# A graph network on one core: the features of layer 0's first convolution turned through HBM, and the plan ordered anew

## The chip, the cores and the metric

The kernel runs on one core of a Trainium2 chip. The metric is device time in microseconds (us), the median of several runs; lower is better. The core has a matrix engine (TensorE, "PE" in the profile; "PEld" is its loading of weights), a vector engine (VectorE, "DVE"), a scalar engine (ScalarE, "ACT"), GpSimd ("POOL"), and a queue engine (SyncE, "SP") that issues most transfers. Each engine works through its own instructions in order, and waits at semaphores for the others.

## The reference

Sixteen graphs of 1024 nodes with 128 features each pass through four layers. Each layer normalises its input, takes `relu` of it, computes a graph operation with the dense 1024 x 1024 adjacency, and adds the result to its input. All is float32.

```python
def _adapt_conv(h, edge_weight, W, b, is_last):      # layer 0: three of these in a row
    h = h @ W + b
    norm = jnp.linalg.norm(h, axis=-1, keepdims=True)
    nh = h / jnp.maximum(norm, EPS)
    cos = jnp.einsum('bij,bkj->bik', nh, nh)
    ew = edge_weight * cos
    h = jnp.einsum('bpq,bqc->bpc', ew, h)
    if not is_last:
        h = jax.nn.relu(h)
    return h
```

Layer 1 multiplies the features by the adjacency and applies two dense matrices. Layer 2 is an attention whose scores are the `tanh` of a sum of two numbers, one of each node. Layer 3 is an attention whose scores come from a product of features with features, symmetrised, masked by the adjacency, with a softmax, and three gates after it.

## The kernel before

**Tiles.** A graph's 1024 nodes are 8 blocks of 128. The features lie with nodes on the partitions (`h`, 128 x 1024: 8 blocks side by side), and, where TensorE has to contract over features, turned, with features on the partitions (`hT`, `hTn`, `hnT`). `hT` is what a convolution's projection `h @ W` reads (`project`, groups `psP`); `hTn` is the turned `h`, both sides of the product `cos` (groups `sq`).

**Turning features** is done in two ways. `flipped` (line 1221 on) transposes 4 blocks at a time on TensorE into a bank of PSUM (`flip`, line 1164), and ScalarE copies the bank to SBUF (`evict`, line 1217): 8 transposes and 2 copies for a graph's features. `squares` (line 1168 on) does it without TensorE: one DMA stores the features in HBM (512 KB), four DMAs (one for each group of 32 partitions) fetch them so that every 32 x 32 square lies where its transpose belongs, and one VectorE instruction transposes the squares in place:

```python
        op("DMA", 3.6, [d], [dst], fetch, lat=2.4)
        dve(V(N), [dst], [dst], lambda: nc.vector.transpose(dst.t[:, 0:N], dst.t[:, 0:N]), True)
```

Before the change, layer 0's normalised input is turned by `squares` in graphs 2 to 15, layer 3's in graphs 1 to 13; all of layer 0's `hTn` are turned by `flipped`, three in a graph.

**The square product.** `Square` computes only the upper triangle of `cos`, row by row (8 rows, 2 halves each: `sq`). ScalarE keeps blocks of it (`above`, line 1387), and TensorE transposes them into the rows below (line 1365). In the middle graphs the quarter that lies furthest below the diagonal comes through HBM instead (`send`): VectorE transposes 32 x 32 squares (line 1377), a DMA stores two rows of blocks (`by_hbm`), four fetch them at their places (`got`). VectorE then multiplies each row by the norm and the adjacency (`ew`, line 1584), and TensorE accumulates (`acc`, lines 1417 and 1428).

**The adjacency** is loaded twice for each graph: as it stands (`adjL`) for layer 1, and turned, through the same 32 x 32 squares (`adjT`, line 1504), for the others.

**The order of the work.** Nothing is issued as the Python code runs. Every step is an `Op` with an engine, a cost, the buffers that it reads and writes, and a rank; the class `Plan` puts all steps of all sixteen graphs into one order, which is then emitted engine by engine. The rank is `batch * PERIOD + due`, with `due` from the table `TIMES`; the table names a step by layer, engine and tile ("00 PE ps": the first convolution's transposes on TensorE), with entries of their own for the first two graphs (`<0`, `<1`) and the last two (`>1`, `>0`), and one set for all others. `order` walks through time: it finds the step that can start first, and of the steps of that engine that can start within `WINDOW` of it takes the one with the lowest rank. Steps of up to `AHEAD` = 2 graphs after the oldest unfinished one may be started, so three graphs are in the works at once. `POOLS` says how many buffers there are of each sort, `KINDS` how many of them a kind of tile may hold, in all and for graphs after the oldest. The order of every engine's instructions, SP's transfers too, is therefore fixed when the program is built, and is the same from one middle graph to the next.

Of the kernel before, what the change touches and what calls it, by code (L numbers as in the profile page):

```python
# [18 lines left out]
D = 128  # L19
# [36 lines left out]
class Plan:  # L56
# [78 lines left out]
    def order(self):  # L135
# [11 lines left out]
        done, oldest = [], 0  # L147
        while ready:
# [4 lines left out]
            found = []  # L153
# [25 lines left out]
            if not found:  # L179
                stuck = [b.name for o in ready if o.batch == oldest for b in o.new]  # L180
                raise RuntimeError(f"no slot for any of {stuck}")
            first = min(found, key=lambda f: f[0])
            at, o = min(
                (f for f in found if f[1].engine == first[1].engine and f[0] <= first[0] + self.window),
                key=lambda f: f[1].rank,
# [35 lines left out]
def tile_adj_preln(  # L221
# [30 lines left out]
    B = x.shape[0]  # L252
# [9 lines left out]
    FLAGS = set("CabcdkxhyzTGmrHWMD3")  # L262
# [61 lines left out]
    for load_it in first:  # L324
# [13 lines left out]
        "adjT": ("adjT", 16, 16), "adjL": ("adjL", 5, 5), "x": ("x", 3, 3), "w4": ("big", 9, 6),  # L338
        "chunk": ("big", 9, 8), "above": ("above", 2, 2), "got": ("got", 1, 1), "ps": ("bank", 6, 7),
        "acc": ("bank", 6, 8), "small": ("small", 9, 12), "row": ("row", 2, 4), "hbm": ("hbm", 3, 2),  # L340
        "hrow": ("hrow", 2, 1), "mask": ("mask", 5, 5), "dot": ("dot", 10, 8),
    }
    PERIOD, AHEAD, WINDOW = 144.89, 2, 0.05

    TIMES = {
        "T DMA raw <0": [45.7, -38, -16.15, 49.25, 9.05, 10.9, 32.75, 4.4],
        "T PE raw <0": [6.9, 8.55, 10, 14.35, 31.1, 9.5, 16.55, 15.55, 20.15, 29.15, 25.45, 37.8, 42.75,
            38.2, 41.55, 44.35],
        "T ACT adjT <0": [8.65, 14, 10.4, 13.35, 16.4, 15.35, 19.25, 20.5, 24.5, 31.15, 33.75, 39, 40.6,
            41.5, 42.7, 45],  # L350
        "T DVE su <0": [52.25],
        "x DMA x <0": [45.65, -6.9],
        "0 DVE st <0": [5.1, 5.15],
        "0 DVE mv <0": [7.1],
        "0 POOL rstd <0": [8.05],
        "0 DVE nb <0": [9.85],
        "0 DVE hn <0": [9.9],
        "0 ACT hn <0": [14],
        "0 PE ps <0": [11.15, 11.3],
        "0 ACT hT <0": [9.25, 12.15],  # L360
        "00 PE psP <0": [33.35, 27.4],
        "00 DVE h <0": [14.25, 12.85],
        "00 PE ps <0": [15.25, 16.1],
        "00 ACT hTn <0": [16.35, 17.25],
        "00 ACT sq <0": [15.5, 19.1],
        "00 DVE ss <0": [15.65, 13.1, 14],
        "00 POOL rn <0": [19.5],
        "00 PE sq <0": [-5, 18.3, 16.7, 19.75, 11.5, 20.4, 14.65, 23.15, 33.4, 31.25, 7.35, 35.7, 33.35,
            37.35, 43.9, 44.5, 41.1, 42.65, 44.4, 43.4, 46.85, 50.85],
        "00 ACT above <0": [19.15, 22.8, 21.35, 22.05, 26.55, 25.8, 31.25, 34.7, 39.05, 45],  # L370
        "00 DVE ew <0": [21.45, 23.5, 21.35, 27.95, 26.1, 24.4, 27.8, 32.75, 38.1, 37.65, 36.45, 43.6, 45.35,
            49.5, 51.65, 54.95],
        "00 PE acc0 <0": [22.5, 43.85, 23.7, 25.85, 30.2, 29.2, 31.65, 31.95, 37.65, 39.45, 47.5, 52.7, 56.2,
            52, 66, 57.2],
        "00 POOL params <0": [24.3, 29.3, 33.35, 36.35, 43.25, 47.85, 33.2],
        "00 DMA params <0": [61.4],
        "00 DVE params <0": [64.75, 67.4, 70.15, 85.4, 74.55],
        "00 PE params <0": [66.15, 67.95, 73.25],
        "00 ACT hT <0": [58.75, 57.25],
        "01 PE psP <0": [54.9, 58.45],  # L380
        "01 DVE h <0": [75.3, 78.3],
        "01 PE ps <0": [81.6, 78.7],
        "01 ACT hTn <0": [77.4, 78.4],
        "01 ACT sq <0": [77.25, 77.9],
        "01 DVE ss <0": [79, 80.5, 81.8],
        "01 POOL rn <0": [81.95],
        "01 PE sq <0": [79.6, 81.15, 81.35, 82.85, 82, 80.95, 84.25, 83.4, 91.3, 87.25, 87.6, 90.65, 91.05,
            95.35, 96.35, 96.45, 95.45, 100.65, 101.75, 96.05, 102.9, 103.05],
        "01 ACT above <0": [81.4, 81.55, 86.1, 87.45, 85, 83.2, 87.3, 92.15, 98.35, 101.95],
        "01 DVE ew <0": [85.3, 83.45, 84.6, 85.3, 86.25, 88.95, 88.25, 89.9, 92.55, 92.5, 96, 96.25, 92.05,  # L390
            102.9, 97.2, 103.55],
        "01 PE acc0 <0": [80.2, 85.15, 89.3, 85.15, 91.9, 92.8, 93.45, 93.7, 94.5, 99.15, 97, 102.1, 101.35,
            103.8, 102.25, 104.9],
        "01 ACT hT <0": [101.95, 110.3],
        "02 PE psP <0": [105.75, 103.9],
        "02 DVE h <0": [107.35, 108.3],
        "02 PE ps <0": [108.45, 108.35],
        "02 ACT hTn <0": [109, 111.65],
        "02 ACT sq <0": [107.85, 109.6],
        "02 DVE ss <0": [110.25, 110.9, 110.4],  # L400
        "02 POOL rn <0": [113.3],
        "02 PE sq <0": [112.75, 113.5, 114.4, 119.4, 115.05, 119.85, 119.1, 119.35, 123.15, 122.15, 121.3,
            129.65, 125.8, 128.95, 127.85, 133.25, 126.35, 130.55, 133.1, 121.6, 133.1, 132.85],
        "02 ACT above <0": [114.15, 115.55, 116.15, 115.7, 117.85, 121.6, 120.6, 122.3, 130.4, 132.1],
        "02 DVE ew <0": [114.9, 115.55, 117.6, 118.45, 119.95, 119.55, 122.7, 122.8, 125.7, 129.1, 129.8,
            131.05, 110.6, 135.15, 124.75, 128.75],
        "02 PE acc0 <0": [114.95, 117.95, 120.2, 117.3, 125.7, 127.15, 125.35, 133.65, 126.15, 130.35, 136,
            133.45, 139.25, 135.55, 138.7, 136.1],
        "02 DVE x <0": [134, 137.25],
        "T DMA adjT <1": [-121.95, -133.95, -119.1, -112.25, -140.55, -203.7, -102.2, -133.55],  # L410
        "T DVE adjT <1": [-117.5, -112.15, -108.9, -105.1, -100.5, -89.9, -92.65, -88.65],
        "T ACT adjT <1": [-114.75, -105.3, -107.95, -101.4, -98, -62.65, -86.35, -86.05],
        "1 DVE st <0": [140.75, 141.25],
        "1 DVE mv <0": [143.55],
        "1 POOL rstd <0": [143.15],
        "1 DVE nb <0": [145.8],
        "1 DVE hn <0": [141.7],
        "1 ACT hn <0": [147.25, 147.4],
        "1 DVE x <0": [160.65, 167.6, 169.75],
        "1 DMA adjL <0": [58.65, 63.6, 66, 162.05, 89.6, 149.8, 153.1, 154.2],  # L420
        "1 DVE adjL <0": [87, 75.3, 80.25, 90.3, 81.9, 154.55, 159.15, 169.4],
        "1 PE acc1 <0": [147.9, 148.75, 149.6, 150.6, 151.35, 152.45, 155, 153.5, 156.1, 144.25, 158.5,
            157.4, 159.55, 156.6, 160.1, 163.85],
        "1 ACT g <0": [161.65, 162.5],
        "1 PE py <0": [163.05, 164.6, 165, 164.15],
        "1 ACT y1 <0": [163.5, 163.25, 168.05, 164.1],
        "1 PE py2 <0": [157.3, 166.9],
        "2 DVE st <0": [169, 170.15],
        "2 DVE mv <0": [172.3],
        "2 POOL rstd <0": [173.3],  # L430
        "2 DVE nb <0": [174.9],
        "2 DVE hn <0": [172.65],
        "2 ACT hn <0": [176.55, 179.7],
        "2 PE ps <0": [205.85, 174.4],
        "2 ACT hnT <0": [180.85, 180.1],
        "2 DVE alone <0": [57.7],
        "2 DVE x <0": [179.05, 214.1, 221.35],
        "2 PE psP <0": [180.65, 182.15, 187.2],
        "2 ACT h <0": [206.2, 185.8, 182.6],
        "2 DVE hrow <0": [183.15],  # L440
        "2 PE pf <0": [185.5],
        "2 ACT hfl <0": [185.45],
        "2 PE pt <0": [199.4],
        "2 ACT sr <0": [182.75],
        "2 DMA sd <0": [186.45],
        "2 DMA s1 <0": [187.05],
        "2 DVE h <0": [184.3],
        "2 ACT e2 <0": [192.75, 195.95, 191.7, 194.45, 196.3, 200.05, 196, 198.85, 200.4, 201.9, 201.95,
            200.1, 203.75, 206.4, 209.5, 205.15],
        "2 DVE e2 <0": [196.9, 196.3, 195.65, 195.05, 199.65, 194.1, 200.3, 199.6, 201.55, 203.65, 201.25,  # L450
            202.3, 207.55, 209.4, 208.6, 208.15],
        "2 PE acc2 <0": [198.15, 201.7, 197.55, 200, 200.45, 199.35, 203, 201.85, 200.95, 203.85, 202.7,
            201.6, 201.1, 203.55, 206.3, 212.65, 207.85, 206.55, 207.15, 208.8, 211.5, 209.85, 210.05, 212.15],
        "2 DVE rden <0": [209.55, 213.7, 212.8, 214.4],
        "3 DVE st <0": [215.4, 207.25],
        "3 DVE mv <0": [210],
        "3 POOL rstd <0": [221.85],
        "3 DVE nb <0": [203.4],
        "3 DVE hn <0": [208.15],
        "3 ACT hn <0": [221.15, 224.35],  # L460
        "3 PE ps <0": [236.25, 224.2, 241.4, 227.7],
        "3 ACT hnT <0": [221.55, 224.2],
        "3 PE pg <0": [242.5, 229.05],
        "3 ACT gT <0": [225.95, 242.2],
# [1055 lines left out]
    def layer0(b, xt, aT, prepared):  # L1520
# [7 lines left out]
        rn = None  # L1528
# [594 lines left out]
```

## Time and profile before

| | |
|---|---|
| median of 3 runs | 2393.26 us (2389.92 to 2393.75) |
| the profiled execution | 2391.87 us |
| its span, first to last instruction | 2390.1 us |
| TensorE clock granted | 0.997 |
| busy: TensorE, VectorE, ScalarE, GpSimd | 2355.8, 2023.5, 1454.3, 247.2 us |
| TensorE instructions | 11689 |
| transposes of `h` into `ps_hTn` | 384, mean 276 ns each |
| HBM read, written | 220.16 MB, 77.13 MB |

Durations overlap on TensorE: a matrix product's row in the profile lasts from its start until its last result is out, while the next one has started already. A float32 product appears as two passes, a transpose as one. What a TensorE instruction takes from the engine is the distance from its start to the next one's, called pitch below.

### The profile page before, as it was taken

The numbers are of one execution on the slowest core, as the hardware profiler recorded it, in microseconds if no ns is written. First come the engines' busy times: TensorE is split into PE (matmuls) and PEld (weight loads), VectorE is DVE, ScalarE is ACT, GpSimd is POOL, SyncE is SP. The second block draws the span as 40 slices with busy tenths as digits, with TensorE's granted clock in tenths as the row PEclk, the third lists the DMA queues.
The fourth block names the chain that finished last, engine by engine and source line by source line (L and its number), as shares of the span: only waits on it lengthen the run. The fifth ranks groups of instructions, "written<-read, shape, count | busy, mean of one in ns | idle before, by whom it ended". The sixth has DMA issues, their size and how long they took to land.

```text
span 2390.1 us, 35188 instructions
## 1 busy us (share of the span) xinstructions
PE 2355.8 (99%) x11689; PEld 1565.0 (65%) x11689; DVE 2023.5 (85%) x5556; ACT 1454.3 (61%) x2589; POOL 247.2 (10%) x168
## 2 busy tenths in 40 slices
PE   8999999999999999999999999999999999999997
PEld 5568566675767657566575766757666575765764
DVE  6668798888989989898888989989899888887676
ACT  6325765756566565755756667565765756655375
POOL 3001010100101101010100101001011100100012
PEclk9999999999999999999999999999999999999999
DMA  9331938758595775948769486785957758155000
GB/s 195 86 106 45 176 89 166 152 110 173 111 170 135 132 167 117 169 114 160 158 110 182 99 170 138 128 173 108 167 131 141 161 113 159 45 89 124 11 17 18
DMA packets 1243941, 299.61 MB, mean 125 GB/s; under 512 B 1049976, under 2 KB 1225216, under 8 KB 1243760
## 3 DMA queue, kind: packets, MB, share of 16 engines
q1 hardware_dynamic: 1223600, 286.67, 60.3%
q10 hardware_dynamic: 19264, 9.70, 1.4%
q8 instruction: 92, 1.51, 0.3%
q0 software_dynamic: 896, 1.01, 0.2%
q14 instruction: 89, 0.73, 0.1%
HBM read 220.16 MB, written 77.13 MB: 124 GB/s over the span
## 4 chain that ended last, share of the span: by engine, by line
PE 93%; DVE 3%; ACT 2%; DMA 1%; SPq 1%; issue 0%; DVEq 0%; ACTq 0%
PE acc L1417 36%; PE sq L1355 20%; PE acc L1428 18%; PE psP L1195 5%; PE sq L1365 4%; PE py L1646 2%; PE py L1205 2%; PE ps_hTn L1164 1%; PE pg L1205 1%; PE psN L1195 1%; SPq L1504 1%; PE ps_h3T L1164 1%; DVE h L1239 1%; PE ps_hnT L1164 1%; DVE ew L1584 0%; DVE x L1239 0%
## 5 line engine op out<-in xcount | busy, mean ns | idle before, releaser
L1417 PE MATMUL acc<-ew,h 128*128 128x512 f32 x1024 | 481.0, 595 | 2.6 <-DVE ew L1584 2.5
L1584 DVE SCALAR_TENSOR_TENSOR ew<-sq,rn,adjT 128x512 f32<-128x512 f32 x612 | 435.5, 738 | 56.0 <-PE sq L1365 27.9
L1355 PE MATMUL sq<-hTn 128*128 128x512 f32 (+3 forms) x1152 | 435.2, 487 | 0.2 <-ACT hTn L1217 0.2
L1387 ACT COPY above<-sq 128x384 f32<-128x384 f32 (+3 forms) x432 | 166.3, 393 | 364.1 <-PE sq L1365 231.7
L1417 PEld LDWEIGHTS acc<-ew,h 128*128 128x128 f32 x1024 | 183.5, 191 | 180.2 <-issue 135.7
L1355 PEld LDWEIGHTS sq<-hTn 128*128 128x128 f32 x1152 | 197.8, 191 | 150.8 <-issue 103.0
L1428 PEld LDWEIGHTS acc<-h,ew 128*128 128x128 f32 x2048 | 245.5, 192 | 29.2 <-issue 26.0
L1428 PE MATMUL acc<-h,ew 128*128 128x128 f32 x2048 | 253.2, 275 | 0.2 <-DVE ew L1584 0.2
L1417 PE MATMUL acc<-e,hs 128*128 128x512 f32 x512 | 246.1, 597 | 2.9 <-DVE e L1890 2.9
L1428 PEld LDWEIGHTS acc<-h,e 128*128 128x128 f32 x2048 | 233.0, 192 | 15.1 <-DVE e L1758 8.7
L1428 PE MATMUL acc<-h,e 128*128 128x129 f32 x2048 | 234.3, 275 | 3.5 <-DVE e L1758 3.4
L1417 PE MATMUL acc<-adjL,hn 128*128 128x512 f32 x512 | 231.1, 593 | 0.1
L1157 POOL TENSOR_TENSOR rstd<-ve,mhalf 128x8 f32<-128x8 f32 x64 | 104.8, 1637 | 1096.2 <-DVE ve L1276 1040.6
L1849 DVE CUSTOM_DVE_ANT_0 e<-mask,sq 128x512 f32<-128x512 int8 x204 | 136.0, 680 | 91.1 <-ACT above L1387 74.7
L1515 ACT ACTIVATE adjT<-adjT 128x1024 f32<-128x1024 f32 x120 | 126.5, 1054 | 100.9 <-DVE adjT L1512 75.9
L1365 PEld LDWEIGHTS sq<-ident,above 128*128 128x128 f32 x960 | 124.0, 141 | 77.2 <-issue 54.2
L1890 DVE TENSOR_TENSOR e<-e,adjT 128x512 f32<-128x512 f32 x248 | 163.9, 682 | 11.3 <-ACT e L1881 11.1
L1365 PE MATMUL sq<-ident,above 128*128 128x128 f32 x960 | 173.3, 273 | 0.0
L1758 DVE SCALAR_TENSOR_TENSOR e<-adjT,e 128x512 f32<-128x512 f32 x256 | 162.3, 696 | 5.8 <-ACT e L1754 5.1
L1417 PEld LDWEIGHTS acc<-adjL,hn 128*128 128x128 f32 x512 | 94.8, 190 | 107.5 <-issue 92.9
L1377 DVE STREAM_TRANSPOSE above<-sq 128x512 f32<-128x512 f32 x208 | 144.7, 705 | 20.3 <-PE sq L1355 19.2
L1838 ACT ACTIVATE mask<-adjT 128x1024 int8<-128x1024 f32 x112 | 117.9, 1054 | 59.2 <-DVE peak L1849 59.0
(163 smaller groups left out, 3645.0 us busy)
## 6 DMA issues: line engine op xcount, KB each, us to landing
adjL<-in_adj_dram SPq DMA_DIRECT2D x128, 512.0 KB, 4.8
adjT<-in_adj_dram SPq DMA_DIRECT2D x480, 128.0 KB, 3.7
by_hbm<-above SPq DMA_DIRECT2D x104, 512.0 KB, 3.7
got<-by_hbm SPq DMA_DIRECT2D x416, 128.0 KB, 2.9
s<-sd SPq DMA_DIRECT2D x15, 512.0 KB, 3.7
out_dram<-z ACTq DMA_DIRECT2D x15, 512.0 KB, 4.1
d_hT<-hn SPq DMA_DIRECT2D x14, 512.0 KB, 3.2
hT<-d_hT SPq DMA_DIRECT2D x56, 128.0 KB, 3.0
```

The lines of the kernel that those rows point to most:

```text
L1195: nc.tensor.matmul(dst.t[:, (c - lo) * n : (c - lo + 1) * n], cols(srcT.t, c), w, start=True, stop=True)
L1355: lambda: nc.tensor.matmul(dst.t[:, (first - lo) * P :], cols(leftT.t, j), span(rightT.t, first, hi), start=True, stop=True),
L1365: nc.tensor.transpose(cols(dst.t, r), cols(above.t, p), ident)
L1377: lambda: nc.vector.transpose(span(above.t, p, p + 4), read.t),
L1387: lambda: nc.scalar.copy(span(above.t, p, p + hi - first), read.t[:, (first - lo) * P :]),
L1417: lambda s=s, lo=lo, hi=hi: nc.tensor.matmul(acc[s].t, cols(h.t, at, w), span(ew.t, lo, hi), start=(j == 0), stop=(j == NB - 1)),
L1428: nc.tensor.matmul(a.t[:, (c - lo) * n : (c - lo + 1) * n], cols(ew.t, c), h.t[:, at * w : at * w + n], start=(j == 0 and c == lo), stop=( ...
L1515: lambda t=t, c=c: nc.scalar.activation(t.t, t.t, AF.Copy, accum_out=su.t[:, c : c + 1]),
L1584: lambda view=view, ew=ew, rn=rn, j=j, lo=lo, hi=hi: nc.vector.scalar_tensor_tensor(by_block(span(ew.t, lo, hi), D, 4), view(), rn.t[:, j ...
L1758: lambda e=e, j=j, lo=lo, hi=hi: nc.vector.scalar_tensor_tensor(span(e.t, lo, hi), span(aT[j].t, lo, hi), 0.0, span(e.t, lo, hi), op0=ALU. ...
L1849: lambda e=e, view=view, mask=mask, peak=peak, s=s, lo=lo, hi=hi: nc.vector.tensor_tensor_reduce(by_block(span(e.t, lo, hi), D, 4), by_blo ...
L1890: lambda e=e, j=j, lo=lo, hi=hi: nc.vector.tensor_mul(span(e.t, lo, hi), span(e.t, lo, hi), span(aT[j].t, lo, hi)),
```

## The change

The first convolution's `hTn` is made by `squares` instead of `flipped` in graphs 2 to 15 (flag `n`; the test `"nop"[i] in FLAGS and b > 1` was there before). Graphs 0 and 1, and the second and third convolution of all graphs, keep `flipped`. The plan is ordered anew: other limits in `KINDS` for the planner, another `PERIOD`, all due times in `TIMES` replaced; the number of buffers (`POOLS`) is the same. Where two engines can start at the same moment the planner now takes the one that comes first in `LATENCY`. Two further flags (`w`, `K`) are named in the code and not set.

```diff
+        rows = {e: i for i, e in enumerate(self.LATENCY)}
...
-            first = min(found, key=lambda f: f[0])
+            first = min(found, key=lambda f: (f[0], rows[f[1].engine]))
...
-    FLAGS = set("CabcdkxhyzTGmrHWMD3")
+    FLAGS = set("CabcdkxhyzTGmrHWMD3n")
...
-        "adjT": ("adjT", 16, 16), "adjL": ("adjL", 5, 5), "x": ("x", 3, 3), "w4": ("big", 9, 6),
-        "chunk": ("big", 9, 8), "above": ("above", 2, 2), "got": ("got", 1, 1), "ps": ("bank", 6, 7),
-        "acc": ("bank", 6, 8), "small": ("small", 9, 12), "row": ("row", 2, 4), "hbm": ("hbm", 3, 2),
-        "hrow": ("hrow", 2, 1), "mask": ("mask", 5, 5), "dot": ("dot", 10, 8),
+        "adjT": ("adjT", 16, 16), "adjL": ("adjL", 5, 5), "x": ("x", 3, 3), "w4": ("big", 11, 5),
+        "chunk": ("big", 13, 11), "above": ("above", 2, 2), "got": ("got", 1, 1), "ps": ("bank", 8, 7),
+        "acc": ("bank", 8, 7), "small": ("small", 7, 18), "row": ("row", 5, 6), "hbm": ("hbm", 3, 3),
+        "hrow": ("hrow", 1, 1), "mask": ("mask", 5, 5), "dot": ("dot", 6, 11),
     }
-    PERIOD, AHEAD, WINDOW = 144.89, 2, 0.05
+    PERIOD, AHEAD, WINDOW = 145.06, 2, 0.05
...
-        "00 PE psP": [-87.3, -102.4],
-        "00 ACT hTn": [-83.9, -84.95],
+        "00 PE psP": [-95, -133.3],
+        "00 DMA d": [-82.95],
+        "00 DMA hTn": [-88.45],
+        "00 DVE hTn": [-68.05],
...
-        if "D" in FLAGS and b > 1:
+        if "D" in FLAGS and b > (0 if "w" in FLAGS else 1):
...
-                if "M" in FLAGS and b >= B - 2:
+                if "K" in FLAGS or "M" in FLAGS and b >= B - 2:
```

In the changed program, a middle graph's new store stands on SP between the store and the fetches of the layer 3 features of the graph two before it, and its four fetches behind those; the VectorE transpose stands behind layer 3's bias additions of that earlier graph.

## The prediction

> **What bounds the kernel now.** I read the page's busy table first, then the chain of work that ended last, then stretches of the span, then one graph row by row.
>
> ```profile
> PE 2355.8 (99%) x11689; PEld 1565.0 (65%) x11689; DVE 2023.5 (85%) x5556; ACT 1454.3 (61%) x2589; POOL 247.2 (10%) x168
> ...
> PE 93%; DVE 3%; ACT 2%; DMA 1%; SPq 1%; issue 0%; DVEq 0%; ACTq 0%
> ```
>
> TensorE carries 93% of the chain. The chain in order of time shows the same piece at the same place of every middle graph:
>
> ```profile
> 616.86 14.29 PE acc L1428 x128
> ...
> 761.14 14.29 PE acc L1428 x128
> ```
>
> So a middle graph takes 761.14 − 616.86 = 144.28 us. The view by stretches (us, then busy PE, PEld, DVE, ACT, POOL, clock, DMA share, GB/s) tells where TensorE is not busy:
>
> ```profile
> 0.00:40.00 40.00, 29.89 (x154) 20.72 (x154) 20.67 (x65) 30.54 (x63) 16.00 (x27) 1.00 1.04 206
> 40.00:184.30 144.30, 141.10 (x638) 88.28 (x639) 97.38 (x245) 45.99 (x100) 18.02 (x17) 0.99 0.46 104
> 184.30:328.60 144.30, 142.70 (x736) 96.35 (x735) 122.25 (x343) 104.09 (x177) 12.09 (x7) 1.00 0.53 111
> ...
> 616.86:761.14 144.28, 144.23 (x714) 95.60 (x713) 128.34 (x351) 90.70 (x160) 13.32 (x8) 1.00 0.71 142
> ...
> 2204.00:2390.10 186.10, 168.44 (x906) 116.79 (x905) 133.33 (x400) 106.50 (x189) 29.00 (x14) 0.97 0.05 17
> ```
>
> Of 34.3 us without TensorE work, 10.1 lie in the first 40 us, 4.8 in the next two stretches, 17.7 in the last 186 us; a middle graph has 0.05. Busy overlaps, so I count the middle graph by pitch (start to start) instead: its timeline has 188 passes of 512 columns at 0.4295 us (2.58 us for six), 402 of 128 to 131 at 0.1117 (14.29 for 128), 16 of 384 at 0.32, 16 of 256 at 0.215, and 89 transposes. The transposes' pitch:
>
> ```profile
> 657.91 1.04 PE L1164 MATMUL ps_h3T<-ident,h 128*128 128x128 f32 x8
> 658.78 1.02 PE L1205 MATMUL pg<-hnT,wg 128*128 128x512 f32 x2
> ```
>
> Eight take 658.78 − 657.91 = 0.87 us, 0.109 each. The sum is 80.7 + 44.9 + 5.2 + 3.4 + 9.7 = 143.9 us: of 144.28, only 0.3 to 0.4 us is waiting. In the middle, TensorE work is the time.
>
> **What the Trainium skill says.** "TensorE: Matmul & The Clock Gate", Part 4: PE-mode transpose, gives about 275 ns for a 128x128 transpose inside a kernel. The trace agrees as to duration (276 ns below), but its pitch is 109 ns, and only the pitch leaves the bound. "Perfetto Trace Analysis", Identifying the Most-Contended Engine, says the same: busy share is no good measure for TensorE. "VectorE: DVE Perf Modes", The three transpose paths: VectorE transposes within 32x32 blocks only, so the blocks must be moved by DMA; that is what the trace's `hT` does. "DMA: Bandwidth & Descriptors", Anatomy of one DMA: some 2 us fixed, mostly completion; here 2.4 to 4.0 us to landing.
>
> **The change part by part.** The group that it cuts, and the existing twin of what it adds (last line: us from issue to landing):
>
> ```profile
> L1164 PE MATMUL ps_hTn<-ident,h 128*128 128x128 f32 x384 | 55.9, 276 | 3.2 <-DVE h L1542 2.6
> ...
> L1217 ACT ACTIVATE hTn<-ps_hTn x96: 578/597/625, 16.3 to 2231.3; 128x512 f32<-128x512 f32 x96
> ...
> L1186 DVE STREAM_TRANSPOSE hT<-hT x14: 1232/1235/1237, 110.8 to 2071.6; 128x1024 f32<-128x1024 f32 x14
> ...
> DMA to landing us min/median/max: 2.4/3.0/4.0
> ```
>
> - *TensorE.* 384 transposes are 16 graphs x 3 convolutions x 8. The first convolution of 14 graphs goes: 112 transposes x 0.109 = 12.2 us less. The rest of its instructions is the same in number.
> - *ScalarE.* 28 evictions x 0.597 = 16.7 us less, on an engine busy 61%: worth nothing by itself.
> - *VectorE.* 14 x 1.235 = 17.3 us more. A middle graph goes from 128.3 to 129.6 of about 143.4 us, 90%. In the changed order it stands just before layer 3's first row of graph b−2, where VectorE now idles 2.11 us for a ScalarE copy (658.94 + 0.16 to 661.21). Worth nothing while that hole stays; if the cover goes, at most 1.24 us a graph.
> - *SP and DMA.* Per graph one store of 512 KB and four fetches of 128 KB. SP now:
>
> ```profile
> 627.28 0.38 SPq L1173 DMA_DIRECT2D d_hT<-hn  x1
> 630.50 2.45 SPq L1181 DMA_DIRECT2D hT<-d_hT  x4
> 644.88 0.38 SPq L1173 DMA_DIRECT2D d_hnT<-hn  x1
> 648.14 2.29 SPq L1181 DMA_DIRECT2D hnT<-d_hnT  x4
> 650.62 0.77 SPq L1397 DMA_DIRECT2D by_hbm<-above  x1
> ```
>
> The new store stands between `d_hnT` and the fetch of `hnT`, in the 2.9 us in which SP only waits for `d_hnT` to land: free. The new fetches stand behind `hnT`'s and hold up the send of graph b−1's third square by about 2.4 us, to some 653 us on this clock. But the new order issues both sends of that square before either fetch; now the second send (657.29) waited behind the first fetch. By these rows the second fetch then ends issuing near 662 instead of 663.3: no loss.
>
> *Is the round trip hidden?* The new chain: projection done near 644.8, `h` added on VectorE by 645.8, store, `hnT`'s fetches to 650.4, its own to 652.8, 3.0 us to land: 655.8. Two consumers. The VectorE transpose: in the changed order VectorE has between the second `h` addition and it 3 reductions x 0.68, 4 block transposes x 0.71, 8 scalings x 0.7, `hnT` 1.24, three additions of 1.5 together and a small one: about 13.5 us, so it is reached near 659.3, 3.5 us after the data. The first square on TensorE: the pitches of what stands between the projection and it add to 36.9 us in every graph from 3 to 13 (38.8 before, transposes included), far more than 12 to 15. Graph 2 has 75, graphs 14 and 15 have 38 and 44.
>
> - *The new order.* Slots are the same, the planner's limits and due times are new. Other covers, in pitch, middle graph before and after: smallest from a square's row to the accumulation that uses it 1.8 and 1.6 us (second smallest 2.2 and 1.7); from layer 2's last accumulation to layer 3's projection 23.95 and 25.68. One shrinks where there is little: the first convolution, from the last row sent through HBM to the first accumulation that needs it back, 13.1 and 12.2 us. Now:
>
> ```profile
> 731.93 1.41 DVE L1584 SCALAR_TENSOR_TENSOR ew<-got,rn,adjT 128x512 f32<-128x512 f32 x2
> ...
> 733.38 1.02 PE L1417 MATMUL acc<-ew,h 128*128 128x512 f32 x2
> ```
>
> The scaling is done at 731.93 + 0.75 = 732.7 and its product used at 733.38: some 0.5 us over, with a hand-over of 0.2 us, if the data landed only just before. With 0.9 us less cover, up to 0.4 us a graph is lost in 12 graphs: 0 to 5 us, or nothing if the data landed earlier. I take 1. At both ends the order differs in detail; the last 33 us of TensorE work (graph 14's gate projections and graph 15's layer 3) come in nearly the same order. I take zero for both ends, with 5 us either way, about a seventh of the 34.3 us there.
>
> **Sum** against the profiled execution: span 2390.1 − 12.2 + 1 = 2378.9; its own time, 1.77 longer, 2391.87 − 11.2 = 2380.7. The median of the runs is 2393.26, 1.39 above that execution, so 2382 (−0.5%). This measurement can tell about 0.2%, 4.8 us.
>
> **Rivals.**
> 1. *The gain stays, but the ends lose.* For: the start (15 us without work, waiting for loads) and the tail were planned anew, and nothing carries over from one order to another there. Against: the tail's order is nearly the old one. Loss 5 to 14 us: 2387 to 2396, about 2390.
> 2. *The new wait decides: slower.* Place: VectorE is in order, and behind the new transpose stand layer 3's first peaks and the scalings of graph b−1's fetched rows, which TensorE waits for. If `hTn` lands later than 659.3 here, VectorE stops. Each us beyond costs up to a us in each of 14 graphs; it cancels the gain at 0.87 us a graph past all cover, and shows as slower at 1.2, that is landing some 5 us later than I work out. For: DMA busy share is 0.71 and rises by about 0.04. Against: the slowest landing of the twin is 4.0. At 2 us a graph: 2382 + 28 = 2410.
> 3. *The ends gain too.* The same 34.3 us may shrink: 2377 to 2369, about 2373.
> 4. *The change does not do what it says:* in the changed program the store, four fetches and transpose stand in graphs 2 to 15. Excluded.
>
> **How the numbers follow.** Forecast 0.67, its own range 2377 to 2387 (5 us for the ends). Rival 1 0.14, half of it past 2388.5, where it counts as the same. Rival 2 0.08: slower 0.06, the same 0.01, faster 0.01. Rival 3 0.11. Faster 0.67 + 0.07 + 0.01 + 0.11 = 0.86, same 0.08, slower 0.06. The range 2375 to 2389 leaves out most of rival 2, half of rival 1 and half of rival 3.
>
> **What would show it.** A middle graph of 143.4 to 143.5 us; TensorE instructions 11577; `ps_hTn` x272, a stream transpose of `hTn` x14 with no DMA wait ahead of it on VectorE; stretches without TensorE work of 30 to 38 us in all, none in the middle. Wrong if a middle graph is above 143.8, or VectorE or TensorE waits for `hTn`, or the first 184 or last 186 us have clearly more idle time.

## The result

The kernel after takes 2388.45 us, the median of 14 runs (2387.24 to 2392.26); the kernel before, run on the same chip between them, 2390.2 us (2388.45 to 2393.75). The ratio is 0.9993, interval 0.9984 to 1.0001: no difference that these runs can tell. The forecast was 2382, 0.5% faster. Its range (2375 to 2389) holds the time, but by luck: it was laid out from the three runs known then (2393.26), and fourteen runs put the kernel before 3 us lower. As shares of the time before, the range ended at 0.9982 and the measured ratio is 0.9993; and by the prediction's own sign (wrong if a middle graph takes more than 143.8 us) it is wrong, as shown below. An outcome of "the same" had been given a chance of 0.08. The question of what follows is where ten of the twelve microseconds went.

The page of the kernel after, the busy table and the chain of work that ended last:

```profile
PE 2349.2 (98%) x11577; PEld 1548.5 (65%) x11577; DVE 2029.0 (85%) x5570; ACT 1435.5 (60%) x2561; POOL 246.8 (10%) x168
...
PE 85%; DMA 5%; SPq 4%; ACT 3%; DVE 3%; issue 1%; DVEq 0%; ACTq 0%
```

TensorE has the 112 instructions less that were counted, and yet its share of the chain fell from 93% to 85%: what ends last now runs through transfers (5%), SP's issuing (4%) and ScalarE. The span is 2387.7 us, 2.4 less than before; the profiled execution took 2389.48.

The groups of what was cut and what was added (busy us and mean ns, then the idle time ahead of them on their engine):

```profile
L1169 PE MATMUL ps_hTn<-ident,h 128*128 128x128 f32 x272 | 41.9, 275 | 0.0
...
L1191 DVE STREAM_TRANSPOSE hTn<-hTn 128x1024 f32<-128x1024 f32 x14 | 17.3, 1236 | 0.1
```

The fourteen transposes on VectorE wait 0.1 us in all: the round trip itself is hidden, as forecast.

The view by stretches answers the forecast's main number (us, then busy PE, PEld, DVE, ACT, POOL, clock, DMA share, GB/s):

```profile
0.00:40.00 40.00, 30.87 (x163) 22.16 (x164) 22.59 (x68) 31.57 (x66) 15.99 (x27) 1.00 1.05 213
40.00:184.30 144.30, 139.70 (x618) 86.56 (x617) 95.12 (x241) 44.13 (x95) 16.37 (x16) 0.98 0.48 105
184.30:328.60 144.30, 142.57 (x726) 95.11 (x725) 120.95 (x342) 104.69 (x179) 13.66 (x8) 1.00 0.58 114
642.86:787.16 144.30, 143.81 (x704) 94.40 (x704) 128.91 (x353) 89.29 (x158) 13.36 (x8) 1.00 0.80 150
787.16:932.17 145.01, 143.73 (x704) 94.38 (x704) 128.67 (x353) 89.39 (x158) 13.36 (x8) 1.00 0.79 149
2204.00:2387.70 183.70, 168.39 (x912) 116.44 (x911) 130.87 (x400) 106.85 (x190) 28.81 (x14) 0.98 0.06 17
```

A middle graph takes 144.3 and 145.0 us here; from 499.02 to 1942.63, ten graphs, it is 144.36 on average, where 143.4 to 143.5 was forecast and 144.28 was measured before. And it holds 0.5 to 1.3 us without TensorE work, where before it was 0.05. The DMA share rose from 0.71 to 0.80, twice the 0.04 forecast.

TensorE's waits in the kernel after, by what it waited for (us in all, times, longest):

```profile
PE acc L1422 <- DVE ew L1589: 8.0, 8, 4.3
...
PE psP L1200 <- ACT hT L1222: 3.2, 13, 0.3
PE acc L1433 <- DVE ew L1589: 3.2, 5, 1.0
```

Before, the wait for `ew` ahead of the first line's accumulation was 2.5 us, that for `hT` 0.5 (once), and that of the last line 0.2. More than half of the first line is one wait at 70 us, at the start of the program (4.3 us, where before there was one of 2.3); the middle has the rest.

**An account of TensorE's time.** Idle time in the profile leaves out hand-overs and the tail of overlapping instructions. So I laid TensorE's instructions in their order end to end, each with its pitch (0.859 us for a product of 512 columns, 0.2234 for one of 128, 0.1095 for a transpose), and took the running sum from the actual starts. Each step by which the difference grows is a wait, and its place is known. The work (with the last 10.7 us of the span, after TensorE's last instruction, counted in) is then the span less all waits: 2348.9 us before and 2336.6 after, 12.3 less, which is the forecast's 12.2. The waits, in us, by place (columns: up to 495 us; then to 1950 us, eleven third convolutions, in the turning chain of the third convolution, ahead of the accumulation of rows that came back from HBM in the third convolution, in the first one, and elsewhere; from 1950 us on):

```
kernel          median  ratio to before           span    to 495  chain  rows 3rd  rows 1st  other  end
before          -       -                         2390.1  24.7    3.0    0         0         0      13.1
after           2388.45 0.9993 [0.9984, 1.0001]   2387.7  27.3    7.1    2.7       3.5       0      10.7
no_trips        2386.37 0.9985 [0.9978, 0.9991]   2383.9  24.7    6.7    0         5.3       0.3    10.5
fill_wait       2390.04 1.0000 [0.9992, 1.0008]   2388.4  25.6    2.3    2.0       4.3       0.4    12.1
fill_busy       2395.36 1.0026 [1.0016, 1.0036]   2393.8  25.8    7.0    3.0       3.5       0      12.8
put_back        2393.18 1.0008 [1.0000, 1.0016]   2393.0  27.8    2.0    0.6       4.8       0.3    10.5
old_cut         2390.32 1.0006 [0.9998, 1.0014]   2390.1  25.4    11.2   0         0         2.4    13.9
fill_real       2398.91 1.0040 [1.0027, 1.0053]   2396.2  28.6    10.8   3.8       3.9       0.2    12.2
fill_real2      2397.61 1.0029 [1.0018, 1.0041]   2393.8  28.3    4.5    5.5       2.9       3.4    12.6
sends_first     2388.03 0.9991 [0.9983, 1.0000]   2385.8  28.7    6.7    0         0         3.6    10.2
sends_first2    2387.09 0.9986 [0.9980, 0.9993]   2384.2  27.3    6.8    0.1       2.1       0.9    10.4
reordered       2393.41 1.0015 [1.0008, 1.0022]   2391.7  28.1    10.4   0.2       1.1       3.5    11.6
reordered2      2392.94 1.0016 [1.0009, 1.0022]   2391.5  29.2    4.4    3.7       2.3       3.5    11.9
split_copy      2385.30 0.9976 [0.9966, 0.9987]   2382.6  27.2    4.6    0.6       1.5       1.4    10.8
```

The columns sum to within 0.7 us of all waits. The waits of before and after close the account: the start +2.6, the chain +4.1, the rows +2.7 and +3.5, the end −2.4 make +10.5 (9.9 with the waits under 0.06 us that the columns leave out), against 12.3 us of work. Some cautions: each row is one execution; the start differs by up to 3 us between executions of one and the same order (no_trips, fill_wait, fill_busy, put_back and the kernel after have the same order there, and 24.7 to 27.8); a step of 0.1 us that falls inside a group of products can be counted in the next column, so that the columns of the middle are good to some 0.4 us. The runs below were made on four chips, each beside the kernel before, whose median there was 2389.5 (no_trips, fill_wait, fill_busy, old_cut), 2389.7 (fill_real, sends_first, reordered), 2389.9 (fill_real2, sends_first2, reordered2) and 2391.8 us (put_back, split_copy): the ratios compare across chips, the medians only roughly.

So there are three suspects in the middle: a chain in the third convolution that the removed transposes used to fill; the third convolution's rows, held up by the new fetches; the first convolution's rows.

### The profile page after: what moved, and what is told of

Read it like the earlier page. It is cut to its first block, busy times and chain, and to the rows that moved or that the text cites. A ratio compares the mean times of both kernels' runs of the same rounds, so it can differ in the third digit from the quotient of the medians.

```text
span 2387.7 us, 35098 instructions
## 1 busy us (share of the span) xinstructions
PE 2349.2 (98%) x11577; PEld 1548.5 (65%) x11577; DVE 2029.0 (85%) x5570; ACT 1435.5 (60%) x2561; POOL 246.8 (10%) x168
## 4 chain that ended last, share of the span: by engine, by line
PE 85%; DMA 5%; SPq 4%; ACT 3%; DVE 3%; issue 1%; DVEq 0%; ACTq 0%
PE acc L1422 33%; PE sq L1360 18%; PE acc L1433 17%; PE psP L1200 6%; PE sq L1370 4%; DMA by_hbm<-above 2%; PE py L1210 2%; DMA got<-by_hbm 2%; PE py L1651 2%; SPq L1413 1%; SPq L1509 1%; PE ps_hTn L1169 1%; PE pg L1210 1%; DVE ew L1589 1%; DMA adjT<-in_adj_dram 1%
## 5 line engine op out<-in xcount | busy, mean ns | idle before, releaser
L1422 PE MATMUL acc<-ew,h 128*128 128x512 f32 x1024 | 486.4, 597 | 8.0 <-DVE ew L1589 8.0
L1422 PE MATMUL acc<-e,hs 128*128 128x512 f32 x512 | 241.1, 594 | 1.3 <-ACT hs L1904 0.8
L1517 DVE STREAM_TRANSPOSE adjT<-adjT 128x1024 f32<-128x1024 f32 x120 | 148.6, 1239 | 8.8 <-DMA adjT<-in_adj_dram 8.4
```

Source lines behind the costliest of these rows:

```text
L1422: lambda s=s, lo=lo, hi=hi: nc.tensor.matmul(acc[s].t, cols(h.t, at, w), span(ew.t, lo, hi), start=(j == 0), stop=(j == NB - 1)),
L1517: dve(V(N), [t], [t], lambda t=t: nc.vector.transpose(t.t, t.t), True)
```

## Experiments

**The chain.** In the kernel before, TensorE's rows at the third convolution of a middle graph were these (start, us, last column the count):

```profile
642.01 2.90 PE L1195 MATMUL psP<-w,hT 128*128 128x128 f32 x24
644.75 1.74 PE L1164 MATMUL ps_hTn<-ident,h 128*128 128x128 f32 x12
646.33 1.88 PE L1355 MATMUL sq<-hTn 128*128 128x512 f32 x4
```

The third convolution's features have to go through a chain there: the last accumulation, ScalarE's copy `hT`, the projection `psP`, VectorE's addition `h`, the transpose `ps_hTn`, ScalarE's copy `hTn`, the square. From one TensorE step to the next the chain costs a copy or an addition on another engine and two hand-overs, and TensorE needs other work meanwhile. Of the 12 transposes, 8 are the next graph's first convolution's: the ones that the change removes. In the kernel after:

```profile
786.31 0.60 PE L1169 MATMUL ps_hTn<-ident,h 128*128 128x128 f32 x4
787.16 2.94 PE L1200 MATMUL psP<-w,hT 128*128 128x128 f32 x24 [0.25 <-ACT hT L1222]
789.94 0.60 PE L1169 MATMUL ps_hTn<-ident,h 128*128 128x128 f32 x4
790.38 1.98 PE L1360 MATMUL sq<-hTn 128*128 128x512 f32 x4
```

Four transposes take 0.44 us, so TensorE could start the projection at 786.75; it starts at 787.16, when the copy is there. That 0.41 us, 0.10 ahead of the projection's second pass and 0.09 in the square recur in every middle graph. The test is to put idle work of known size once into the gap and once elsewhere (fill_wait, fill_busy; four transposes are 0.44 us, over 12 graphs 5.3 us). The edit is fill_wait's; fill_busy has `i == 1`, the second convolution, where TensorE does not wait. They write a bank that the projection then overwrites.

```diff
     def emit():
+        for _ in range(extra):
+            nc.tensor.transpose(dst.t[:, 0:P], ident, ident)
...
-po = project(hT, lo, hi, w0[i], pp)
+po = project(hT, lo, hi, w0[i], pp, 4 if i == 2 and s == 1 and 2 <= b <= 13 else 0)
```

> The changed kernel with four more transposes of a constant on TensorE just ahead of the third convolution's second projection in graphs 2 to 13 (48 x 0.109 = 5.3 us of TensorE work; the result is the same). Theory, filler: TensorE stands 0.41 us a graph there, waiting for ScalarE's copy, so the work costs nearly nothing: 0 to 1 us, about 2389. Rival, every us of TensorE work counts: 5.3 us, about 2394.

> The same four transposes ahead of the second convolution's second projection in graphs 2 to 13, where TensorE does not wait. Both theories: 5.3 us more, about 2394. If it costs nothing either, TensorE is not the bound of the middle graphs at all.

Measured: fill_wait 2390.04 us, its span 0.7 above the kernel after; fill_busy 2395.36, its span 6.1 above. The same 48 transposes cost 5.4 us more in one place than in the other. In fill_wait the wait is gone from TensorE's rows, the four idle transposes (first line) standing in its place:

```profile
785.06 0.60 PE L1200 MATMUL psP<-ident 128*128 128x128 f32 x4
785.49 2.92 PE L1202 MATMUL psP<-w,hT 128*128 128x128 f32 x24
788.25 0.60 PE L1169 MATMUL ps_hTn<-ident,h 128*128 128x128 f32 x4
788.69 3.48 PE L1362 MATMUL sq<-hTn 128*128 128x512 f32 x8
```

The chain's waits fell from 7.1 to 2.3 us. So work in this gap is all but free, which also says what taking work out of it is worth in this order.

put_back fills it with eight transposes, four there and four between the two projections of the next graph (`i == 0 and 3 <= b <= 14`), where the removed ones used to stand: nearly the TensorE work of the kernel before, in the order of the kernel after.

> The changed kernel with eight transposes a graph put back on TensorE in the gap of the third convolution, graphs 2 to 13: four ahead of psP half 1 as in fill_wait, four between the next graph's two projection halves, ahead of ps_hTn half 1. They write a bank that the projection overwrites, and nothing reads them. 96 x 0.109 = 10.5 us of TensorE work. If the gap there (0.60 us a graph of waiting) swallows its part, 12 x 0.60 = 7.2 us of it costs nothing and the time rises by 3.3 us: 2391.7 us (2390 to 2393). If work counts in full, 2399.

Measured: 2393.18 us on a chip on which the kernel before took 2391.8; ratio 1.0008, 0.15% or 3.6 us above the kernel after's 0.9993, where a rise of 3.3 was expected (in spans 5.3, of which 0.5 at the start; the intervals of the two ratios touch). 10.5 us of work came for a third to a half of their length.

The other side of the same test: the order of the kernel before, with nothing but these 112 transposes left out (old_cut). ScalarE copies `h` where it copied the transposes, so that every engine's sequence stays; the first convolution's square is then computed from features that are not turned.

```diff
+            if cut:
+                pe((hi - lo) * TR, [blk(src, lo, hi, w)], [p], lambda: None)
+                act(S((hi - lo) * P), [p], [blk(dst, lo, hi)],
+                    lambda lo=lo, hi=hi: nc.scalar.activation(span(dst.t, lo, hi), span(src.t, lo, hi), func))
+                continue
...
-else flipped(h, f"hTn_{k}")
+else flipped(h, f"hTn_{k}", cut=i == 0 and b > 1)
```

> The kernel before, in its own order, with the 112 transposes of the first convolution left out in graphs 2 to 15; ScalarE copies h itself (the result is another), nothing goes through HBM. Theory, filler: those transposes stood between the third convolution's second projection and its transposes, which wait for VectorE; a part of the time freed is given back there, about half: 5 us less (3 to 8), about 2385. Rival, TensorE is the bound everywhere: 12.2 us less, about 2378.

Measured: 2390.32 us, ratio 1.0006 (0.9998 to 1.0014), span 2390.1: nothing at all is gained. Both expectations were too low. TensorE's rows:

```profile
643.69 0.82 PE L1164 MATMUL ps_hTn<-ident,h 128*128 128x128 f32 x4
644.35 1.02 PE L1362 MATMUL sq<-hTn 128*128 128x512 f32 x2
645.90 1.77 PE L1362 MATMUL sq<-hTn 128*128 128x512 f32 x4 [0.53 <-ACT hTn L1217]
```

The transposes gone, TensorE comes to the square 0.9 us sooner and waits there for ScalarE's copy of the second half: 1.0 us a graph, 11.2 in the eleven graphs against 3.0. Leaving out the transposes, and them alone, gains nothing in that order. But ScalarE's rows show that not all of this wait is the chain's own:

```profile
644.23 0.62 ACT L1230 ACTIVATE hTn<-h 128x512 f32<-128x512 f32 x1
644.75 0.61 ACT L1568 ACTIVATE sq<-h 128x512 f32<-128x512 f32 x1
645.27 0.57 ACT L1217 ACTIVATE hTn<-ps_hTn 128x512 f32<-128x512 f32 x1
```

TensorE waits for the last of these, and it stands behind a copy that old_cut kept and the change removes (the first line); ScalarE works without a gap there. Without that copy the last one could come up to 0.52 us sooner (645.27 to 644.75), so that by an estimate from these rows up to 5.7 of the 11.2 us are ScalarE's kept copies. No run leaves out both, transposes and copies, in the old order; what that would have gained stays open. In the order after, the copy `hT` that TensorE waits for starts 0.2 us after the accumulation is done (786.51 to 786.31): there the wait is the chain's.

**The rows.** Does the round trip's traffic hold TensorE up? no_trips leaves out the store and the four fetches of `hTn` and lets VectorE transpose `h` in their stead, in the same order; its features are not the turned ones.

```diff
-lambda: nc.sync.dma_start(d.t.rearrange("(c p) f -> p c f", p=P), by_block(src.t, w)[:, :, 0:D]), lat=2.2,
+(lambda: nc.sync.dma_start(d.t.rearrange("(c p) f -> p c f", p=P), by_block(src.t, w)[:, :, 0:D])) if trip else (lambda: None), lat=2.2,
...
-op("DMA", 3.6, [d], [dst], fetch, lat=2.4)
+op("DMA", 3.6, [d], [dst], fetch if trip else (lambda: None), lat=2.4)
...
-dve(V(N), [dst], [dst], lambda: nc.vector.transpose(dst.t[:, 0:N], dst.t[:, 0:N]), True)
+dve(V(N), [dst], [dst], lambda: nc.vector.transpose(dst.t[:, 0:N], (dst if trip else src).t[:, 0:N]), True)
```

> The changed kernel, order as it is, with the store and the four fetches of the first convolution's turned features left out in graphs 2 to 15 (VectorE turns the squares of h in place of the fetched ones, so the result is another). Theory, late rows: the 70 new transfers delay the rows that come back through HBM (got), and TensorE waits for them at the first and third convolution of some middle graphs, some 6 us in all; these waits go, the wait of 0.41 us a graph before the third convolution's second projection stays: about 2382 us (2380 to 2384). Rival, the new order itself leaves too little cover: the waits stay, 2387 to 2390.

Measured: 2386.37 us, 0.0008 or 2 us below the kernel after (the intervals overlap; 3.8 by the spans, of which 2.6 at the start): between the two theories. The third convolution's rows wait no more (2.7 us to 0), but the first convolution's wait longer (5.3 us), and the chain's waits stay (6.7). So the late rows are two losses. That of the third convolution is the round trip's, and SP's rows in the kernel after show how:

```profile
792.99 3.06 SPq L1186 DMA_DIRECT2D hnT<-d_hnT  x4
796.16 2.64 SPq L1186 DMA_DIRECT2D hTn<-d_hTn  x4
798.89 2.01 SPq L1402 DMA_DIRECT2D by_hbm<-above  x2
804.70 5.86 SPq L1413 DMA_DIRECT2D got<-by_hbm  x8
```

The send stands behind the new fetches, as forecast, and then lands in 5.8 us (798.89 to 804.70), beside the fetches' small packets, where it took 4.2 before (650.62 to 654.84). The first scaling of fetched rows follows on VectorE, and TensorE's accumulation on that:

```profile
814.34 0.75 DVE L1589 SCALAR_TENSOR_TENSOR ew<-got,rn,adjT 128x512 f32<-128x512 f32 x1 [1.75 <-PE sq L1360]
```

```profile
815.14 1.16 PE L1433 MATMUL acc<-h,ew 128*128 128x128 f32 x8 [1.03 <-DVE ew L1589]
```

The scaling comes 24.0 us after the third square's first product (790.38); before, 20.6 us (646.33 to 666.93). (The idle time ahead of the scaling is put down to TensorE's square; the chain of work has the transfer `got` there, 809.74 for 4.18 us, that is until 813.92.)

The first convolution's loss is not the round trip's. The queue's table (packets, MB, share of 16 engines) for the kernel before, for no_trips, which moves the same packets, and for the kernel after:

```profile
q1 hardware_dynamic: 1223600, 286.67, 60.3%
```

```profile
q1 hardware_dynamic: 1223600, 286.67, 65.3%
```

```profile
q1 hardware_dynamic: 1296400, 301.35, 67.6%
```

The new order alone made the same packets take 5 points more; the round trip added 2.3 to 4.4 (fill_wait, fill_busy and put_back, with the transfers of the kernel after in its order, have 68.1% to 69.7%; old_cut, with those of the kernel before, has 60.0%). And the time from issue to landing of what goes through HBM for the square (last number), before and in no_trips:

```profile
by_hbm<-above SPq DMA_DIRECT2D x104, 512.0 KB, 3.7
got<-by_hbm SPq DMA_DIRECT2D x416, 128.0 KB, 2.9
```

```profile
by_hbm<-above SPq DMA_DIRECT2D x104, 512.0 KB, 4.1
got<-by_hbm SPq DMA_DIRECT2D x416, 128.0 KB, 4.2
```

Fetches land 1.3 us later in the new order without any added transfer. Part of it can be placed: the rows of the third square and of layer 3's, which the new order fetches eight transfers in a row (`got` x8 above) and the old one four and four, land in 4.3 to 4.4 us on average instead of 2.7 to 3.0 (a third of them have a landing in the trace). The last fetches of the first convolution's rows, four in a row in both orders, land in 3.8 instead of 3.2. What delays these I did not find out.

**Can both be mended?** sends_first takes the steps of the kernel after in another order on their engines, nothing else: on SP the fetches of `hTn` behind both sends and fetches of the third square, its VectorE transpose behind four scalings; on TensorE one product of the first convolution 1.7 us earlier, which its second send waits for. In this diff and the next ones a line names the engine, the step that is moved and its new place; b is the graph, and a number behind it the convolution.

```diff
+("DMA", hTn of graph b+1, behind the second got of b_2)
+("DVE", hTn of graph b+1, behind ew_b_2_6, first half)
+("PE", sq_b_0_3_1, one accumulation ahead of py of graph b-1, second part)
```

> The changed kernel with the fetches of hTn moved on SP behind both sends and both fetches of the third square's rows (its VectorE transpose moved behind four scalings that use them), graphs 2 to 13, and with the first convolution's square sq row 3 half 1, which the second send waits for, one accumulation and one product (1.7 us) earlier on TensorE, graphs 3 to 13. If the waits ahead of the accumulations (acc0 of the third and of the first convolution, 5.5 us in ten middle graphs of the changed kernel's profile) come from rows sent late in these two places, most of them go: 4 to 6 us, 2383.5 us (2382 to 2385.5). If they come from the transfers' own load on the DMA engines, wherever they stand, the time stays at 2387 to 2390; if hTn now comes too late for VectorE or TensorE, a new wait for it shows and the time goes above 2390.

Measured: 2388.03 us, no better than the kernel after within these intervals, and short of the 4 to 6 us. The waits ahead of both accumulations went, as the first theory has it; but 0.37 us a graph of new ones came: 0.18 in a later row of the third convolution's accumulation, 0.09 in layer 1's `acc<-adjL,hn` and 0.10 in layer 3's `psN`. VectorE now did the 1.24 us transpose between two scalings instead of in a hole; the next run, in which it does not, has the 0.10 alone. sends_first2 leaves VectorE as it was and takes only the first send ahead of the fetches:

```diff
+("DMA", by_hbm_b_2_0, ahead of hTn of graph b+1)
+("PE", sq_b_0_3_1, as above)
```

> A smaller edit than sends_first: on SP only the first send of the third square's rows (by_hbm) goes ahead of hTn's fetches; fetch and VectorE transpose of hTn stay where they were; the first convolution's sq row 3 half 1 1.7 us earlier, as before. If the first send's lateness is what VectorE and TensorE waited for, the waits ahead of acc0 of the third and first convolution (5.5 us in ten middle graphs) go without the new ones of sends_first (0.35 us a graph, put down to the moved transpose): 2384 us (2382 to 2386). If the fetches' load slows the send that runs beside them, so that its landing stays near 5.8 us, the third convolution's waits stay and the time is 2386 to 2388.

Measured: 2387.09 us, ratio 0.9986 (0.9980 to 0.9993), some 1.7 us better than the kernel after by the ratios (whose intervals overlap), 3.5 by the spans. SP's rows and the scaling on VectorE:

```profile
795.19 0.86 SPq L1460 DMA_DIRECT2D by_hbm<-above  x1
796.16 3.52 SPq L1244 DMA_DIRECT2D hTn<-d_hTn  x4
800.19 0.40 SPq L1460 DMA_DIRECT2D by_hbm<-above  x1
800.69 8.18 SPq L1471 DMA_DIRECT2D got<-by_hbm  x8
```

```profile
812.37 0.75 DVE L1647 SCALAR_TENSOR_TENSOR ew<-got,rn,adjT 128x512 f32<-128x512 f32 x1
```

The first send is 3.7 us earlier; it still takes until 800.69, 5.5 us, beside the fetches, so both theories had something: the load is real, and the place in the queue decides whether it matters. Third rows 0.1 us, first rows 2.1.

For the chain, fill_real puts work of the kernel's own into the gap: the next graph's first projection ahead of `ps_hTn`, its VectorE transpose `hT` ahead of the addition of `h`, and the first squares ahead of the second `ps_hTn`, in graphs 2 to 13.

```diff
+("DVE", hT of graph b+1, ahead of h_b_2, first half)
+("PE", psP of graph b+1, first half, ahead of ps_hTn_b_2_0)
+("PE", sq_b_2_0_0, ahead of ps_hTn_b_2_1)
+("PE", sq_b_2_1_0, ahead of sq_b_2_0_1)
```

> The changed kernel with other work of its own put into the gap of the third convolution, in graphs 2 to 13: the next graph's first projection half (psP, 0.89 us) goes ahead of ps_hTn half 0, its VectorE transpose hT ahead of the addition of h, and the first row of the square product (0.86 us, needs only half 0 of hTn) goes ahead of ps_hTn half 1, the second row's first half ahead of the first row's second half. Nothing is added or left out. If the waits there (0.41 + 0.10 + 0.09 us a graph in the changed kernel) are want of work to fill the chain accumulation, ScalarE copy, projection, h, transpose, copy, then 0.4 to 0.5 us a graph comes back in 12 graphs: about 5 to 6 us, 2383 us (2381 to 2385), and the row 'psP <- ACT hT' of the waits is gone. If the late copy of ScalarE is itself the limit and the wait only moves to the next step of the chain, the time stays at 2387 to 2389.

Measured: 2398.91 us, 10 us worse than the kernel after, outside both expectations (five runs). The waits of the chain rose to 10.8 us. ScalarE's rows:

```profile
790.08 0.63 ACT L1624 ACTIVATE sq<-h 128x512 f32<-128x512 f32 x1 [4.76 <-issue]
790.62 0.58 ACT L1280 ACTIVATE hT<-acc 128x512 f32<-128x512 f32 x1
```

The accumulation was done near 789.5, but the copy `hT` stands behind a square of `h`, and `h` was now 1.2 us late because VectorE transposed first. reordered has this and sends_first's edits together:

> Both reorderings together. If the two losses are independent, their gains add: about 10 us below the changed kernel, 2378 us (2376 to 2381), a middle graph of 143.5 us, which is what the prediction of 143.4 to 143.5 counted. If they are one chain (what is saved in one place is waited for in the other), the time is that of the better of the two alone, 2383 us.

Measured: 2393.41 us, between the two runs and again outside both expectations. fill_real2 takes that copy ahead of the square, and the next graph's squares and sums behind what the third square needs; reordered2 has this and sends_first2's edits together:

```diff
+("ACT", hT_b_2, second half, ahead of sq_b_2, first half)
+("ACT", sq of graph b+1, both halves, behind above_b_2, second row)
+("DVE", ss of graph b+1, both halves, behind ew_b_2_3, first half)
```

> fill_real again, with what its trace showed in the way taken out: on ScalarE the copy hT of the accumulation's second half goes ahead of the square of h (sq), which waited for the addition of h that the transpose hT had pushed back by 1.2 us; and the squares and sums (sq, ss) of the next graph go behind the blocks above that the third square needs. If the loss of fill_real (8.5 us more waiting) came from that copy standing behind a late square on ScalarE, the wait ahead of psP half 1 (0.45 us a graph) goes, and the time falls below the changed kernel's: 2383 to 2386, 2385 us. If VectorE or the chain itself is the limit, it stays at 2388 or above.

> Both edits together: their gains add if they are two separate losses: 2380 us (2378 to 2383). If one wait only moves into the other, not below 2384.

Measured: 2397.61 and 2392.94 us, both as the rival has it and not as hoped. The wait ahead of `psP` is gone and the chain's waits are 4.5 us, as the first theory has it, but in fill_real2 the third convolution's rows wait 5.5 instead of 2.7, layer 3's first products 3.4 instead of 0, and the start of the span and its end are each 1 to 2 us longer. VectorE and ScalarE carry the same work in another sequence, and more than was taken off the chain came back at other places where TensorE waits for them. I did not follow each of these further.

What remains is an edit that moves nothing: split_copy is sends_first2 with ScalarE's one copy of 512 columns on the chain made as two of 256, so that the projection starts after the first.

```diff
-nc.scalar.activation(span(dst.t, lo, hi), span(src.t, 0, hi - lo), func, **kw)
+step = (hi - lo) // parts
+for c in range(0, hi - lo, step):
+    nc.scalar.activation(span(dst.t, lo + c, lo + c + step), span(src.t, c, c + step), func, **kw)
...
-evict(acc[s], hT, lo, hi, AF.Relu)
+evict(acc[s], hT, lo, hi, AF.Relu, parts=2 if i == 1 and s == 1 and 2 <= b <= 13 else 1)
```

> sends_first2 with one more edit: ScalarE copies the second half of the second convolution's accumulation (hT, 0.60 us) in two instructions of 256 columns instead of one of 512, in graphs 2 to 13, so that the third convolution's projection can begin after the first; a copy of 256 columns takes 0.37 us (above, in the changed kernel's profile). Nothing else moves on any engine. If TensorE's 0.41 us ahead of psP half 1 is the latency of that copy, the wait falls by 0.23 us a graph, 2.8 us in all: 2384.3 us (2383 to 2386). If something else (VectorE, the bank) sets that moment, the time stays at 2387.

Measured: 2385.3 us, ratio 0.9976 (0.9966 to 0.9987), the lowest of all: 5.7 us below the kernel before, clear of the noise; 4 below the kernel after and 2.4 below sends_first2 by the ratios, whose intervals overlap. ScalarE's rows and TensorE's:

```profile
785.40 0.66 ACT L1282 ACTIVATE hT<-acc 128x256 f32<-128x256 f32 x2
```

```profile
785.19 0.60 PE L1227 MATMUL ps_hTn<-ident,h 128*128 128x128 f32 x4
785.83 2.94 PE L1258 MATMUL psP<-w,hT 128*128 128x128 f32 x24
```

The two halves take 0.66 us together, 0.06 more than one; the projection starts 0.64 us after the transposes instead of 0.85. The wait of 0.41 is 0.20, as expected.

## Why the prediction was wrong where it was, step by step

*TensorE's work.* "112 transposes x 0.109 = 12.2 us less": right, 12.3 by the account.

*"In the middle, TensorE work is the time."* Here the prediction failed. It is true of the kernel before, in which TensorE hardly waited, and it was taken to mean that less work is less time. The step that carried it over was the sum's first term: all 12.2 us were taken off the path, and "0.3 to 0.4 us" of waiting a graph was kept. The 0.3 was small because there was work in every gap, some of it the very transposes to be removed. By pitch alone a full engine and one whose gaps are just filled look alike. To tell them apart I would have had to ask what TensorE does without the eight transposes: the chain from accumulation to square beside which they stood could be read from the trace of before (ScalarE's copy of 0.60 us and two hand-overs ahead of the projection, and so on). The chain took 4.1 of the 12.2 us in the order after. In the order before, with ScalarE's copies kept, waits at the same place take 8.2 (old_cut), and the rest of the gain goes at the start, the end and in layer 3.

*ScalarE's 28 copies: "worth nothing by itself".* Not tested, and doubtful by old_cut's rows: in the order before, one of them stands right ahead of a copy that TensorE waits for once the transposes are gone. A busy share of 61% did not show that.

*The fetches in front of the send: "no loss".* Wrong: 2.7 us. The prediction laid the new issue times end to end and came out 1.3 us ahead of the old ones for the second fetch. It used the durations of an undisturbed send. Counted from the square's first product, the first send was issued 4.2 us later (8.5 us instead of 4.3), where 2.4 had been counted; with the fetches beside it it took 5.8 us instead of 4.2; SP ended issuing the last fetch 20.2 us after that product (810.56 to 790.38) instead of 16.9 (663.27 to 646.33), and the rows' first use came 3.4 us later. The rise of the DMA share was put at 0.04 and was 0.09 in a middle graph. The round trip's own part was not underrated: without it, in no_trips, two middle graphs show 0.80 and 0.75. It is the order that was left out of this sum.

*First convolution's rows: "0 to 5 us, I take 1".* The term was right and its size too small: 3.5 us, and 5.3 without the round trip. The cover shrank by 0.9 us as computed; that transfers land later in the new order was left out. That the later landing is the whole of this loss is not shown.

*The round trip itself:* hidden, as worked out; 0.1 us of waiting on VectorE in 14 graphs, and TensorE nowhere waited for that transpose. The store stands in SP's gap, as counted. VectorE's hole took the transpose.

*Both ends: zero, 5 us either way.* +2.6 and −2.4, within the bounds; the start's part is no more than the scatter between executions.

*The sum.* Forecast span 2378.9, measured 2387.7, 8.8 more: the chain 4.1, the third convolution's rows 2.7, the first's 2.5 above what was taken, the ends 0.2, less 0.6 us of small waits that the columns leave out and 0.1 of work: 8.8.

*The rivals.* The first named the time (2387 to 2396) but not the place: the ends did not lose. The second had the kind of wait (a transfer that comes late stops VectorE, and TensorE behind it) at the wrong tile: `hTn` was in time, the rows whose send it had pushed back were not. No rival said that removed work may have been cover.

## What to carry to other kernels

Before a saving on the busiest engine is counted, ask what that engine would do in those nanoseconds: if the removed instructions stand beside a chain through other engines, they are its cover, and their price is what is left of them after that chain. A run that only leaves the work out, in the old order, asks this before any new path is built; here it gained nothing. It should leave out all that the change would take away, the other engines' part too, or it measures a queue that the change would have shortened. When a chain's latency is what is left, shortening one link without moving anything (a copy in two parts) took half of the wait there away, and filling its gap with work that other engines had to bring forward cost more than it gained.

## What the runs showed that I had not expected

An order of instructions alone changed how long the same 1223600 packets take: 60.3% of the DMA engines' time before and 65.3% in no_trips, with the fetches landing in 4.2 us instead of 2.9 (executions of one order differ by up to 2.1 points). And a ScalarE copy from PSUM splits cheaply: two of 256 columns, of which one alone takes 0.37 us (`above`), follow each other in 0.66 us, against 0.60 for one of 512.
